# Adding a bias row and a layer's output to the residual with accumulating transfers begun on GpSimd

## The chip, the cores and the metric

The kernel runs on one core of one Trainium2 chip. The metric is device time in microseconds of one execution of the whole program. The engines of the core are TensorE (PE in the profile; its weight loads are PEld), VectorE (DVE), ScalarE (ACT), GpSimd (POOL) and SyncE (SP). Sixteen DMA engines move data between the on-chip memory and HBM, and inside the on-chip memory.

## The reference

Four graph attention layers run over `x` of shape (128, 64, 512), fp32, with one adjacency matrix of 64 x 64. Each is added to its input:

```
h = max(layernorm(x), 0);  x = x + layer_l(h)
layer 0: softmax(q k' / 8, masked) v                      8 heads of 64, q = h Wq + bq and so on
layer 1: the same, then @ Wo + bo
layer 2: r = adj' * (q k');  (r / |r| by rows) v          one head
layer 3: o = (masked softmax attention) @ Wp + bp;  o + layernorm(o) * gamma + beta
```

So in layers 0, 1 and 3 a row of 512 numbers (`bv`, `bo`, `beta`) is added to every row of the residual, and in layer 3 the projection's output `o` is added to the residual as well, beside its normalized form.

## The kernel before, in words

The 8192 rows are cut into 16 blocks of 512 rows (`NT` = 4 tiles of 128 partitions). The main loop takes all 16 blocks of layer 0, then those of layer 1, and so on: `n` runs from 0 to 63 with `l, k = divmod(n, 16)`. Between the layers a block's residual lies in HBM (`state`).

For each block, `load_x` brings the rows and `layer_norm` makes the transposed, normalized `hT`. The transposition is in `turn`: a DVE copy that splits the 32-bit words into halves (`z`), a transposing DMA issued on SP (`hp<-z`), and an ACT copy that joins the halves again. Projections are Strassen-like: seven products of 256 x 256 parts in place of eight, with sums of parts made on POOL (`S`, `SO`). `attend` makes scores, softmax and transposed weights (`s`, again with `turn`), and `finish0`, `finish13` multiply them with `v`.

`load_xo` loads the residual block a second time, into `xo`, and adds the row (`row`, a copy of the bias in every partition) with four POOL additions of 128 x 512. In layer 0 DVE then adds the attention's output to `xo`; in layer 1 the output projection adds its parts on DVE and POOL; in layer 3 `tail3` takes the finished output `o` tile by tile: statistics on DVE, `xo + o` on POOL, then on DVE two operations that add the normalized form, then the store. `o` lies in the one buffer named `kT`, which the key projection of another block writes next; the second last block has it in a weight buffer, `w`. The last block has a tail of its own in the main program, with its additions on DVE.

Nothing is issued when it is written in the source. Every operation is recorded as a step (`record`, `add`) with what it reads and writes, and `order` sorts all of them at the end: a list scheduler with a duration for each step from `duration`. Each engine takes the step of lowest rank that is ready by the plan's clock; a step on another engine may use a result `late` ns after its end. `port` and `PORT` model that DVE and POOL share a port. `issue` then writes the instructions in that order, and each engine runs its own list in order, with semaphores between engines. All of them therefore carry line 193 in the profile. Rotating buffers (`Ring`) are chosen while recording, so the order doesn't change them. PSUM has four buffers for projections (`mm`) and two for attention (`so`).

Of the kernel before, what the change touches and what calls it, by code (L numbers as in the profile page):

```python
# [15 lines left out]
ALU = mybir.AluOpType  # L16
AX = mybir.AxisListType

P = 128
G = 64  # L20
D = 512
KC = D // P
HD = 64
NT = 4
# [31 lines left out]
class Plan:  # L56
# [59 lines left out]
    def add(self, eng, calls, reads, writes, busy, late):  # L116
        i = len(self.steps)
        deps = {self.wrote[g] for g in reads | writes if g in self.wrote}
        for g in writes:
            deps |= self.readers.pop(g, set())  # L120
            self.wrote[g] = i
        for g in reads:
            self.readers.setdefault(g, set()).add(i)
        deps.discard(i)
        if eng == "tensor":
            self.products.append(i)
        elif eng == "sync" and len(self.products) >= AHEAD:
            deps.add(self.products[-AHEAD])
        self.steps.append((eng, calls, deps, busy, late))

    def order(self):
        n = len(self.steps)
        wait = [len(s[2]) for s in self.steps]
        users = [[] for _ in range(n)]
        for i, s in enumerate(self.steps):
            for d in s[2]:
                users[d].append(i)

        rank = [i - RUSH * any(v.tensor.name.startswith("mm_") for c in s[1] for v in c[1][1:] if isinstance(v, bass.AP)) for i, s in enumerate(self.steps)]
        ready = [0.0] * n  # L140
        free = {e: 0.0 for e in ("tensor", "vector", "scalar", "gpsimd", "sync")}
        moved = 0.0
        port = 0.0
        soon = {e: [] for e in free}
        here = {e: [] for e in free}
        for i in range(n):
            if not wait[i]:
                heapq.heappush(soon[self.steps[i][0]], (0.0, rank[i], i))
        out = []
        while len(out) < n:  # L150
            best = None
            for e in free:
                while soon[e] and soon[e][0][0] <= free[e]:
                    heapq.heappush(here[e], heapq.heappop(soon[e])[1:])
                if here[e]:
                    at = free[e]
                elif soon[e]:
                    at = soon[e][0][0]
                else:
                    continue  # L160
                if best is None or at < best[0]:
                    best = (at, e)
            at, e = best
            if not here[e]:
                while soon[e] and soon[e][0][0] <= at:
                    heapq.heappush(here[e], heapq.heappop(soon[e])[1:])
            i = heapq.heappop(here[e])[1]
            eng, _, _, busy, late = self.steps[i]
            if e == "sync":
                moved = max(moved, at + 1400) + late / 180  # L170
                late = moved + 600 - at - busy
            elif e == "vector" and late == PORT:
                busy += max(0.0, free["gpsimd"] - at)
                port = at + busy
            elif e == "gpsimd":
                busy += max(0.0, port - at)
            free[e] = at + busy
            out.append((at, i))
            for u in users[i]:
                same = self.steps[u][0] == e  # L180
                ready[u] = max(ready[u], at + busy + (0.0 if same and e != "sync" else late))
                wait[u] -= 1
                if not wait[u]:
                    heapq.heappush(soon[self.steps[u][0]], (ready[u], rank[u], u))
        self.start = {i: at for at, i in out}
        self.span = max(free.values())
        return [i for _, i in sorted(out)]
# [37 lines left out]
def duration(eng, op, aps, a, k):  # L225

    out = aps[0]
    n = out.free_size()
    if eng == "tensor":
        kdim, m = aps[1].partition_size(), aps[1].free_size()  # L230
        if op == "transpose":
            return 109, 200
        pass_ = max(n, P if m > HD else HD) * 0.842
        if m <= HD:
            pass_ = pass_ / (2 if kdim > HD else 4) + 1
        return 2 * pass_, 200
    if eng == "vector":
        n = max([n] + [v.free_size() for v in aps[1:]])
        if op == "bn_stats":
            return 590, 150  # L240
        if n <= HD:
            return 120, 150
        if out.dtype == U16:
            return 0.67 * n, PORT
        fixed = {"scalar_tensor_tensor": 140, "tensor_reduce": 100}.get(op, 85)
        two = sum("PSUM" not in str(v.space) and v.free_size() > HD for v in aps[1:]) > 1
        return fixed + n * 1.01, PORT if two else 150
    if eng == "scalar":
        own = isinstance(k.get("scale"), bass.AP)
        return max(240 + 0.49 * n, (1.32 if out.dtype == U16 else 1.4 if own else 0.95) * n), 170  # L250
    if eng == "gpsimd":
        if n <= HD:
            return (1010 if ALU.pow in a else 310), 120
        return n * (1.82 if n > D else 2.41), 120
    size = (2 if out.dtype == U16 else 4) * n * out.partition_size()
    return 1270 if k.get("transpose") else 520, size


@with_exitstack
def gnn_stack_kernel(  # L260
# [12 lines left out]
    pe, dve, act, gps = plan.tensor, plan.vector, plan.scalar, plan.gpsimd  # L273
# [28 lines left out]

    def dma(dst, src):
        plan.sync.dma_start(dst, src)

    def col(name, src):
        t = const.tile([P, KC], F32, tag=name, name=name)
        dma(t, src.rearrange("(c p) -> p c", p=P))
        return t
# [12 lines left out]
    def source(l, k):  # L322
        return xr[k] if l == 0 else state[l - 1][k]
# [112 lines left out]
    def stats(mv, t, src, nm):  # L436
        st = sm.tile([P, 6], F32, tag="st", name=f"st_{nm}_{t}")
        dve.bn_stats(st, src)
        dve.bn_aggr(mv[:, t, :], st)
# [6 lines left out]
    ready = set()  # L446
# [249 lines left out]
    def pieces(n, xo):  # L696

        l, k = divmod(n, NB)
        for g in range(2):
            at = slice(2 * g, 2 * g + 2)  # L700
            if l in (1, 3):
                yield xo[:, at, :], lambda d, at=at: d[at].rearrange("t p d -> p t d")
            else:
                yield xo[:, at, 0:H2], lambda d, at=at: d[at, :, 0:H2].rearrange("t p d -> p t d")
                for y in range(2):
                    yield (
                        xo[half(y), at, H2:],
                        lambda d, at=at, y=y: d[at, half(1 - y), H2:].rearrange("t p d -> p t d"),
                    )

    def store(n, xo):
        l, k = divmod(n, NB)
        for sb, dr in pieces(n, xo):
            dma(dr(target(l, k)), sb)

    xos = {}

    def load_xo(n):
        l, k = divmod(n, NB)
        xos[n] = p2.tile([P, NT, D], F32, tag="xo", name=f"xo_{n}")  # L720
        for sb, dr in pieces(n, xos[n]):
            dma(sb, dr(source(l, k)))
        yield 4
        if l in xo_row:
            row = R[xo_row[l]]
            for t in range(NT):
                gps.tensor_tensor(xos[n][:, t, :], xos[n][:, t, :], row, ALU.add)
                if t < NT - 1:
                    yield 1
        ready.add(("xo", n))  # L730

    def finish0(n):
# [118 lines left out]
    def tail3(n, o):  # L851

        xo = xos[n]
        mv = sm.tile([P, NT, 2], F32, tag="mv", name=f"mvo_{n}")
        rs = sm.tile([P, NT], F32, tag="rs", name=f"rso_{n}")
        yield 1
        for t in range(NT):
            stats(mv, t, o[:, t, :], f"o{n}")
            gps.tensor_tensor(xo[:, t, :], xo[:, t, :], o[:, t, :], ALU.add)
            yield t % 2  # L860
        pow_mhalf(rs, mv[:, :, 1], LN_EPS, f"o{n}")
        yield 1
        for t in range(NT):
            a = p4.tile([P, D], F32, tag="z", name=f"a_{n}_{t}")
            dve.scalar_tensor_tensor(a, o[:, t, :], mv[:, t, 0:1], R["gam"], ALU.subtract, ALU.mult)
            dve.scalar_tensor_tensor(xo[:, t, :], a, rs[:, t : t + 1], xo[:, t, :], ALU.mult, ALU.add)
            yield 1
        yield 1
        store(n, xo)
# [138 lines left out]
    for n in range(N):  # L1008
        l, k = divmod(n, NB)
# [14 lines left out]
        if l != 2:  # L1024
# [12 lines left out]
            if l == 0:  # L1037
                spawn(load_xo(n), 2)
# [30 lines left out]
    for t in range(NT):  # L1069
# [10 lines left out]
        o, xo = o3[:, t, :], xos[m][:, t, :]  # L1080
        dve.tensor_tensor(o, ps, R["bp"], ALU.add)
        stats(mv, t, o, "last")
        at = slice(t, t + 1)
# [41 lines left out]
```

## Time and profile before

| | us |
|---|---|
| median of 3 runs (lowest, highest) | 2844.2 (2843.95, 2844.62) |
| the profiled execution's own time | 2844.57 |
| span in its trace, first to last instruction | 2842.8 |
| busy in that span: PE | 2828.4 |
| DVE | 2037.6 |
| POOL | 1840.5 |
| ACT | 1248.0 |

The profile's groups are named by what they write and read, with buffer numbers left out: `xo<-xo,row` is the addition of a row to the residual, `hp<-z` a transposing DMA, `so<-v,s` and `so<-s,v` the attention products, `mm<-...` the projections. Weight loads overlap products. Issuing a DMA is not counted as busy time of the engine that issues it; such an entry carries a q (SPq). Matmuls are pipelined and their groups overlap, so that a group's mean duration times its count exceeds its busy time.

### The profile page before, as it was taken

The page shows a single profiled execution, that of the slowest core. Times are in us where ns is not written, and L with a number is a line of the kernel's source. Part 1 is how long each engine was busy: PE and PEld are TensorE (multiplying, and loading weights), DVE is VectorE, ACT ScalarE, POOL GpSimd, SP SyncE. Part 2 cuts the span into 40 slices and gives each one's busy share as a digit, 9 for nine tenths or more (in the row PEclk, how much of TensorE's full clock was granted, in tenths as well). Part 3 has the DMA queues.
Part 4 walks back from the last instruction along what each step waited for, and adds up shares of the span by engine and source line. Part 5 has one row for each costly group of instructions (what it writes and reads, how often), then busy time and mean ns, then how long its engine had stood idle before and what let it go on. Part 6 is the DMA issues. An engine that isn't in the chain of part 4 may idle for free.

```text
span 2842.8 us, 62036 instructions
## 1 busy us (share of the span) xinstructions
PE 2828.4 (99%) x25833; PEld 2471.6 (87%) x25833; DVE 2037.6 (72%) x3104; ACT 1248.0 (44%) x1589; POOL 1840.5 (65%) x1349
## 2 busy tenths in 40 slices
PE   9999999999999999999999999999999999999998
PEld 8878888888888888888888888888888888888887
DVE  7767778876767767667666555555688888778787
ACT  4555555454443534534434343443444444444442
POOL 6555566656766667667677334344678687787796
PEclk9999999999999999999999999999999999999999
DMA  6766666556453533533546565756433433433432
GB/s 158 163 137 156 143 146 134 127 128 163 105 120 80 124 95 82 131 85 86 136 114 156 136 162 143 164 128 157 120 86 94 119 86 95 112 91 96 109 84 66
DMA packets 634890, 342.29 MB, mean 120 GB/s; under 512 B 485232, under 2 KB 566384, under 8 KB 634608
## 3 DMA queue, kind: packets, MB, share of 16 engines
q1 hardware_dynamic: 634608, 338.32, 50.0%
q8 instruction: 202, 3.31, 0.5%
q14 instruction: 80, 0.66, 0.1%
HBM read 152.61 MB, written 69.21 MB: 78 GB/s over the span
## 4 chain that ended last, share of the span: by engine, by line
PE 96%; DVE 3%; issue 0%; POOL 0%; DMA 0%; ACT 0%; POOLq 0%; SPq 0%; DVEq 0%
PE mm L193 88%; PE so L193 8%; DVE z L193 1%; DVE st L193 0%; POOL s L193 0%; DVE u L193 0%; DVE sr L193 0%; DVE kT L193 0%; DMA xin<-in_x_dram 0%; DVE mv L193 0%; DVE w L193 0%; DVE xo L193 0%; ACT xin L193 0%; ACT oT L193 0%; POOLq L1120 0%
## 5 line engine op out<-in xcount | busy, mean ns | idle before, releaser
L193 PE MATMUL mm<-S,w 128*128 128x256 f32 x3584 | 817.2, 380 | 0.0
L193 PEld LDWEIGHTS mm<-S,w 128*128 128x128 f32 x3584 | 679.3, 190 | 93.8 <-issue 1.0
L193 PE MATMUL mm<-hT,w 128*128 128x256 f32 x2688 | 629.9, 380 | 4.0 <-DVE kT L193 3.7
L193 DVE TENSOR_TENSOR u<-mm,s 128x512 f32<-128x512 f32 x414 | 284.9, 688 | 480.1 <-PE mm L193 342.3
L193 PEld LDWEIGHTS mm<-hT,w 128*128 128x128 f32 x2688 | 509.6, 190 | 75.5 <-DVE kT L193 5.3
L193 PE MATMUL mm<-w,S 128*128 128x256 f32 x2048 | 472.8, 381 | 0.0
L193 PEld LDWEIGHTS mm<-w,S 128*128 128x128 f32 x2048 | 385.5, 190 | 53.8 <-issue 0.5
L193 ACT COPY hT<-hp 128x1024 uint16<-128x1024 uint16 x252 | 332.7, 1350 | 90.3 <-DMA hp<-z 90.2
L193 PE MATMUL mm<-w,hT 128*128 128x256 f32 x1536 | 366.4, 381 | 0.0
L193 ACT COPY s<-hp 128x1024 uint16<-128x1024 uint16 x188 | 252.3, 1352 | 204.3 <-DMA hp<-z 197.1
L193 ACT COPY s<-mm 128x512 f32<-128x512 f32 x211 | 123.0, 583 | 490.0 <-PE mm L193 419.0
L193 POOL TENSOR_TENSOR s<-s,mx 128x1024 f32<-128x1024 f32 x96 | 183.3, 1911 | 226.9 <-DVE mx L193 224.9
L193 PEld LDWEIGHTS mm<-w,hT 128*128 128x128 f32 x1536 | 289.2, 190 | 40.2 <-DVE v L193 0.2
L193 POOL TENSOR_TENSOR xo<-xo,row 128x512 f32<-128x512 f32 x192 | 286.1, 1510 | 8.4 <-DMA xo<-in_x_dram 5.7
L193 DVE COPY z<-s 128x1024 uint16<-128x1024 uint16 x188 | 278.2, 1501 | 6.7 <-POOL s L193 6.6
L193 DVE COPY z<-xin 128x1024 uint16<-128x1024 uint16 x252 | 245.3, 988 | 37.6 <-ACT xin L193 34.0
L193 ACT ACTIVATE xin<-xin,nb,rs 128x512 f32<-128x512 f32 x256 | 195.4, 808 | 90.5 <-DVE nb L193 89.9
L193 PE MATMUL mm<-w,SO 128*128 128x256 f32 x992 | 224.3, 379 | 0.0
L193 POOL TENSOR_TENSOR qT<-u,z 128x512 f32<-128x512 f32 x64 | 87.5, 1367 | 202.2 <-DVE u L193 189.8
L193 PEld LDWEIGHTS mm<-w,SO 128*128 128x128 f32 x992 | 188.5, 190 | 25.6
L193 POOL TENSOR_TENSOR s<-s,sr 128x1024 f32<-128x1024 f32 x96 | 187.3, 1963 | 34.2 <-DVE sr L193 32.1
L193 ACT ACTIVATE s<-s 128x1024 f32<-128x1024 f32 (+1 forms) x112 | 108.1, 966 | 200.3 <-POOL s L193 144.3
(98 smaller groups left out, 3667.7 us busy)
## 6 DMA issues: line engine op xcount, KB each, us to landing
xin<-x SPq DMA_DIRECT2D x192, 256.0 KB, 4.0
xo<-x SPq DMA_DIRECT2D x64, 512.0 KB, 4.5
xin<-in_x_dram SPq DMA_DIRECT2D x64, 256.0 KB, 3.2
x<-xo SPq DMA_DIRECT2D x64, 256.0 KB, 2.5
x<-xo SPq DMA_DIRECT2D x128, 128.0 KB, 2.5
x<-xo SPq DMA_DIRECT2D x32, 512.0 KB, 3.0
out_dram<-xo SPq DMA_DIRECT2D x30, 512.0 KB, 3.0
xo<-in_x_dram SPq DMA_DIRECT2D x32, 256.0 KB, 3.2
```

Of the source, the lines that this page charges most:

```text
L193: getattr(getattr(self.nc, eng), op)(*a, **k)
```

## The change

The four row additions of a block become one accumulating DMA of 128 x 4 x 512 elements, issued on GpSimd's queue: `xo += row`, where the row is repeated four times by the access pattern. In `tail3`, the four additions of the output become one accumulating DMA of 128 x 2048 elements, recorded after the statistics of the last tile. The scheduler learns that a DMA may be issued by GpSimd: a step behind it on the same engine waits for its landing if it uses its result, and `duration` gives such a transfer 1100 ns on GpSimd and `2000 + size / 180` ns to landing. Steps of the last block's own tail stay as they are.

```diff
-            eng, _, _, busy, late = self.steps[i]
+            eng, calls, _, busy, late = self.steps[i]
+            moves = calls[0][0] == "dma_start"
+            if e == "gpsimd":
+                busy += max(0.0, port - at)
             if e == "sync":
                 moved = max(moved, at + 1400) + late / 180
                 late = moved + 600 - at - busy
             elif e == "vector" and late == PORT:
                 busy += max(0.0, free["gpsimd"] - at)
                 port = at + busy
-            elif e == "gpsimd":
-                busy += max(0.0, port - at)
...
-                ready[u] = max(ready[u], at + busy + (0.0 if same and e != "sync" else late))
+                ready[u] = max(ready[u], at + busy + (0.0 if same and not moves else late))
...
-    if eng == "gpsimd":
+    if eng == "gpsimd" and op != "dma_start":
...
     size = (2 if out.dtype == U16 else 4) * n * out.partition_size()
+    if "accum_op" in k:
+        return 1100, 2000 + size / 180
     return 1270 if k.get("transpose") else 520, size
...
+    def add(dst, src):
+
+        gps.dma_start(dst, src, accum_op=ALU.add)
...
             row = R[xo_row[l]]
-            for t in range(NT):
-                gps.tensor_tensor(xos[n][:, t, :], xos[n][:, t, :], row, ALU.add)
-                if t < NT - 1:
-                    yield 1
+            add(xos[n], row.unsqueeze(1).to_broadcast([P, NT, D]))
+            yield 3
         ready.add(("xo", n))
...
             stats(mv, t, o[:, t, :], f"o{n}")
-            gps.tensor_tensor(xo[:, t, :], xo[:, t, :], o[:, t, :], ALU.add)
+            if t == NT - 1:
+                add(xo, o)
             yield t % 2
```

## The prediction

> **What bounds the kernel now.** I read the page's engine row first, then the list of PE's waits, then the groups by form, then the timeline of one layer-0 block. The engine row:
>
> ```profile
> span 2842.8 us, 62036 instructions
> PE 2828.4 (99%) x25833; PEld 2471.6 (87%) x25833; DVE 2037.6 (72%) x3104; ACT 1248.0 (44%) x1589; POOL 1840.5 (65%) x1349
> ```
>
> PE is busy for all but 14.4 us of the span. The list of PE's waits (engine, line, waited for: us in total, times, longest) says how little of that is a wait:
>
> ```profile
> PE mm L193 <- DVE kT L193: 3.7, 4, 0.9
> PE mm L193 <- POOL ident masks.py:199: 1.3, 1, 1.3
> ```
>
> All its entries sum to 6.4 us; the rest is the head and the tail. The 3.7 us are four stalls of 0.9 us in layer 3, where DVE, held up beside POOL, emptied a PSUM bank late. So whatever leaves POOL or DVE can give back about 4 us, and anything that makes PE wait is paid in full. The groups that the change touches (busy us, mean ns of one, idle before):
>
> ```profile
> L193 POOL TENSOR_TENSOR xo<-xo,row 128x512 f32<-128x512 f32 x192 | 286.1, 1510 | 8.4 <-DMA xo<-in_x_dram 5.7 <-DMA xo<-x 2.7
> L193 POOL TENSOR_TENSOR xo<-xo,kT 128x512 f32<-128x512 f32 x56 | 80.8, 1472 | 0.0
> L193 POOL TENSOR_TENSOR xo<-xo,w 128x512 f32<-128x512 f32 x4 | 6.3, 1605 | 0.0
> L193 ACT COPY s<-hp 128x1024 uint16<-128x1024 uint16 x188 | 252.3, 1352 | 204.3 <-DMA hp<-z 197.1 <-DVE mv L193 5.8 <-DVE u L193 0.9
> q1 hardware_dynamic: 634608, 338.32, 50.0%
> ```
>
> ACT's copy of a transposed attention tile waits 197 us for the transposing DMA: that DMA is the last step before the attention product. The DMA engines are half busy; by stretches it is 0.63 in layer 0 (42 to 760 us), 0.45 in layer 1 (760 to 1560), 0.38 in layer 3 (2010 to the end). In one layer-0 block (start, length, engine):
>
> ```profile
> 518.32 2.91 SPq L193 DMA_TRANSPOSE hp<-z  x2
> 522.55 4.63 POOL L193 TENSOR_TENSOR xo<-xo,row 128x512 f32<-128x512 f32 x3
> 526.49 2.61 SPq L193 DMA_TRANSPOSE hp<-z  x2
> 531.91 1.37 ACT L193 COPY s<-hp 128x1024 uint16<-128x1024 uint16 x1
> 536.55 2.10 PE L193 MATMUL so<-v,s 64*64 64x64 f32 x128
> ```
>
> The last attention copy ends at 533.28 and the attention product starts at 536.55: a margin of 3.3 us, with the row additions standing among the very transposes that fill it. Measured so in the timeline for each block, the margin is 0.8 to 3.3 us in layer 0 (mean 2.1), 1.8 to 3.5 in layer 1 (2.4), and 0.4 to 3.7 in layer 3 (1.5). PE runs in a fixed order, so a tile later than that stops it.
>
> **What the Trainium skill says.** "DMA: Bandwidth & Descriptors", Anatomy of one DMA (SWDGE path): a transfer begun on GpSimd takes about 2.0 us plus bytes at 436 GB/s. The same page, Issuing engines are not separate DMA queues: transfers of all engines share the same 16 DMA engines and interleave. "Collectives: The Full Stack", The bandwidth ceiling: an add inside the DMA needs two source reads on one read ring and so runs at about half the rate of a copy. "SBUF — State Buffer", Who interferes with whom: GpSimd writes the descriptors through the port it shares with VectorE, so a VectorE copy can hold them up. The trace of before has no transfer begun on GpSimd, so the first and third can't be checked. That DVE copies and POOL block each other it shows: the copy z<-s takes 0.7 us alone and up to 1.9 beside POOL (group mean 1501 ns against 988 for the same copy z<-xin).
>
> **The change, part by part.** *Removed from POOL:* 192 row additions (286.1 us) and 60 output additions (80.8 + 6.3), 373 us of its 1840.5. None ends PE's waits, so nothing comes back there except part of the four stalls of 0.9 us: I count -3 us.
>
> *Added to POOL:* 63 transfers of 1 MB, 48 of the row (16 blocks in each of layers 0, 1 and 3) and 15 of the output. What POOL is held for one is not shown. Below it is bounded by SP's DMA issue, 0.58 us (median); above by the four additions it replaces, 6.0 us. I take 1.1 us, the value by which the changed plan lays its order (69 us in all), against the page's 2.0 us for everything fixed, most of which it puts at completion.
>
> *Landing.* Two reads of 1.05 MB at 436 GB/s are 4.8 us on all 16 engines, so 6.8 us on idle engines (estimate from the two pages). At layer 3's share of 0.38 the 4.8 us stretch to 7.7 and the landing to 9.7 us. The plan assumes 1.1 + 7.8 = 8.9. The bound below is 4.4 us (one read); above I take 15, twice the plan's. Altogether 63 x 4.8 = 302 us of all engines, 50% to about 61%.
>
> *Moved.* Instruction counts on PE, DVE, ACT and SP stay; PE's order changes in few places, mostly neighbouring products swapped. What was spread in four pieces is now one burst, and SP's transposes share the engines with it. Queue by queue:
> - Layer 0: the row transfer stands on POOL just after qT<-u,z, where the block above has its additions (522.55), with the four attention transposes issued from 518 to about 530. The burst takes up to 4.8 us from them; I take 4.1, near the top, because transposes stand before and behind it in SP's queue. Less the margin of 2.1 this is 2.0 us of PE per block, x16 = 32 us. Bounds: 0 (it fits into the idle 37%) and 4.8 - 0.8 = 4, x16 = 64.
> - Layer 1: the row transfer stands before the two s<-s,sr multiplications, so half of the burst is over when the first transpose comes: 2.4 us against a margin of 2.4. I take 0.25 x16 = 4; bounds 0 and 16 x 1.5 = 24. The addition's user, DVE xo<-mm,xo, came 5.9 us after POOL's last row addition before; the transfer starts earlier and covers that.
> - Layer 3, row: the same place, margin 1.5: 0.5 x15 = 8; bounds 0 and 35.
> - Layer 3, output: the transfer waits for all of o. Behind it, DVE has before the first xo<-z,rs,xo: 6 statistics with aggregates at 0.79 us, 4 z<-kT at 0.75, two u<-mm at 0.6, nb: about 9.3 us. Landing at 9.7 leaves DVE waiting 0.4 us; behind it stand qT<-mm,u and the z<-xin copies, PE's next banks and the next block's hT. I take 0.5 x14 = 7; bounds 0 and (15 - 9.3) x14 = 80. The next writer of o's one buffer, ACT kT<-mm, comes some 13 us after o's last write (2505.5 to 2518.4), beyond the landing. The wait for the store falls behind this and hides in SP's idle time (SP waited 490 us for DVE xo).
>
> What covers POOL's 1.1 us is the time that the removed additions left. If it were longer, the s<-s,sr behind it in layers 1 and 3 would be late, and with them the copies, transposes and attention product.
>
> **The sum.** 32 + 4 + 8 + 7 - 3 = +48 us on the profiled execution's 2844.57 (span 2842.8 and 1.8 around it), which lies 0.4 above the median 2844.2: 2892 us.
>
> **The rivals.**
> - *Hidden, not slower.* The bursts fit into the engines' idle time, the margins hold and the stalls of 0.9 us shrink. For it: margins of 2 us everywhere and a DMA share of 0.4 to 0.6. Against: in layer 0 the transfer meets the transposes in every block. It decides where the burst delays the last transpose by less than about 1 us in layer 0. 2841 to 2849 us. Chance 0.14; in a fifth of it just faster by over 0.2%, which would need more than the waits listed, from the ends of the span.
> - *POOL is held longer.* The row transfer is 512 pieces of 2 KB, and DVE's copies shut the port. At 4 us POOL is late by 2.9 in front of s<-s,sr: less margins of 2.4 and 1.5, about 0.5 x16 + 1.4 x15 = 29 us more, and as much again where ve, rs and nb stand behind the output's transfer (1.5 x14 = 21): 2940. At 6 us 2 more per block on 45 blocks: 3030. For it: nothing in this trace prices it. Against: POOL has gained 373 us. Chance 0.26.
> - *The addition is slow in the DMA engines* (landing 13 to 15 us). In layer 3 DVE waits 4 to 6 us x14 with two banks' time (2 us) of it hidden by PE's lead, 28 to 56 us more: 2920 to 2950, and transposes suffer longer, up to 3000. Chance 0.15.
> - *It doesn't do what it says:* excluded for the most part, since the built order has all 63 transfers in place of the 252 additions.
>
> **How the numbers follow.** About 0.2% (5.7 us) is what a measurement can tell from no change. My case (2850 to 2920) has 0.44, hidden 0.14, POOL held 0.26, slow addition 0.15, and 0.01 is left over. Faster 0.03; same 0.11 (the rest of hidden); slower 0.86. The likeliest is 2892. The range reaches from hidden, 2842, to POOL held for nearly 6 us, 3015; about one in ten lies above and one in twenty below.
>
> **What would show it.** Right: PE waits for ACT s<-hp by some 2 us a block in layer 0, few in layer 1; ACT waits longer than 197 us for hp<-z; POOL busy near 1500 us; DMA share up by about 10 points. In layer 3, DVE xo<-z,rs,xo ends less than 1 us after its transfer. Wrong: no new PE waits (hidden); POOL's transfers of several us with s<-s,sr late (second rival); DVE xo waiting many us for xo<-kT (third).

## The result, and the profile after

The changed kernel takes 2891.22 us (median of 4 runs, 2884.75 to 2896.02) against 2844.07 for the kernel before (the three runs above and one more): ratio 1.0164, 95% interval 1.0151 to 1.0176, slower by 47 us. The profiled execution is the shortest of the four, 2884.75 us with a span of 2882.9, so its own account has to explain 40 us and not 47.

The page of the changed kernel, engines and DMA queues:

```profile
span 2882.9 us, 61996 instructions
PE 2840.5 (99%) x25833; PEld 2476.4 (86%) x25833; DVE 1933.2 (67%) x3104; ACT 1241.7 (43%) x1589; POOL 1559.0 (54%) x1160
...
q1 hardware_dynamic: 634608, 338.32, 50.7%
q0 software_dynamic: 27504, 66.06, 13.3%
...
xo<-row POOLq DMA_DIRECT2D x48, 1024.0 KB, 8.4
...
xo<-kT POOLq DMA_DIRECT2D x14, 1024.0 KB, 7.1
```

POOL lost 281 us of work. DVE lost 104 us; its copy `z<-s` fell from 1501 to 1263 ns, less often held up beside POOL. Neither was the bound. The 63 transfers (queue q0) take 13.3% of the DMA engines. Still PE looks 99% busy: its busy time grew by 12 us, most of which the clock explains below.

PE's waits (engine, line, waited for: us in total, times, longest):

```profile
PE mm L194 <- DVE u L194: 7.1, 3, 5.8
PE so L194 <- ACT s L194: 6.0, 3, 3.8
PE mm L194 <- ACT kT L194: 5.2, 2, 4.7
PE mm L194 <- DVE kT L194: 5.0, 2, 3.2
PE mm L194 <- ACT z L194: 3.2, 1, 3.2
PE mm L194 <- ACT hT L194: 2.4, 1, 2.4
```

All entries of the list sum to 34.2 us, against 6.4 before: +27.8. The timeline puts practically all of the new ones before 800 us, in layer 0 and its end; layer 3's four stalls of 0.9 us are gone. Only the second entry is the attention product that I had named. The others are projections whose PSUM bank or operand came late from DVE or ACT. Who held those up, in the waits of layer 0 alone (42 to 770 us):

```profile
ACT s L194 <- DMA hp<-z: 104.4, 34, 10.5
...
DVE z L194 <- DMA hp<-z: 70.8, 22, 11.8
ACT hT L194 <- DMA hp<-z: 62.1, 31, 6.7
```

Before, in layer 0 (42 to 760 us), ACT waited less than half as long for the same DMAs, and DVE 3.1 us in all:

```profile
ACT s L193 <- DMA hp<-z: 43.6, 22, 5.5
...
ACT hT L193 <- DMA hp<-z: 26.9, 24, 3.1
```

The transposes landed late (landing is the moment when all data of a transfer has arrived). In layer 0, first before, then after:

```profile
DMA to landing us min/median/max: 3.0/3.2/6.4
...
DMA to landing us min/median/max: 3.0/3.8/16.3
```

One block shows the whole course (the timeline, engine by engine: start, length, engine, operation, and in brackets the idle time before it and what ended it):

```profile
421.03 1.65 POOL L194 DMA_DIRECT2D xo<-row  x1
...
421.83 8.26 SPq L194 DMA_TRANSPOSE hp<-z  x2
...
431.30 1.89 PE L194 MATMUL mm<-w,hT 128*128 128x256 f32 x8
...
437.63 0.69 DVE L194 COPY z<-s 128x1024 uint16<-128x1024 uint16 x1 [11.78 <-DMA hp<-z]
437.68 1.34 ACT L194 COPY s<-hp 128x1024 uint16<-128x1024 uint16 x1 [10.52 <-DMA hp<-z]
438.24 0.68 DVE L194 TENSOR_TENSOR u<-mm,s 128x512 f32<-128x512 f32 x1
...
438.98 3.78 PE L194 MATMUL mm<-w,S 128*128 128x256 f32 x8 [5.79 <-DVE u L194]
```

POOL begins the transfer at 421; SP needs 8.3 us to issue two transposes, which take 1.2 us each otherwise; ACT stands 10.5 us and DVE 11.8 us before a step that needs a transposed tile or the buffer `z` that the transpose still reads. The PSUM evacuation `u<-mm,s` (it takes a finished product out of its bank) stands behind that step on DVE, and PE stops for 5.8 us.

The last line shows a second cost: eight products in 3.78 us, where eight of the same shape took 1.89 just before the stall. Busy time by stretches (PE busy, PEld, DVE, ACT, POOL, then PEclk, DMA share, GB/s):

```profile
415.00:436.00 21.00, 18.19 (x85) 15.67 (x83) 9.21 (x16) 4.88 (x8) 7.29 (x5) 1.00 1.00 121
437.20:443.90 6.70, 4.92 (x52) 3.73 (x56) 5.00 (x9) 3.28 (x3) 1.26 (x1) 0.50 1.17 167
444.00:470.00 26.00, 26.00 (x324) 22.90 (x317) 20.53 (x30) 14.86 (x20) 17.09 (x12) 1.00 0.51 130
```

PE's clock is granted at half (0.50) after the stall. The clock records show five such stretches, four of 3.4 us and one of 6.8, together 20.5 us at half clock. PE stood still in 2.4 us of these; the 18.1 us in which it worked cost half of that, 9 us. Waits and clock make 27.8 + 9 = 37 of the 40 us. The other 3 lie in PE's busy time (it grew by 12, of which the clock is 9), and I can't place them.

### The profile page after: what moved, and what is told of

It is laid out like the page before. It is cut to its first block, busy times and chain, and to the rows that moved or that the text cites. A ratio compares the mean times of both kernels' runs of the same rounds, so it can differ in the third digit from the quotient of the medians.

```text
span 2882.9 us, 61996 instructions
## 1 busy us (share of the span) xinstructions
PE 2840.5 (99%) x25833; PEld 2476.4 (86%) x25833; DVE 1933.2 (67%) x3104; ACT 1241.7 (43%) x1589; POOL 1559.0 (54%) x1160
## 3 DMA queue, kind: packets, MB, share of 16 engines
q0 software_dynamic: 27504, 66.06, 13.3%
## 4 chain that ended last, share of the span: by engine, by line
PE 91%; DMA 5%; DVE 2%; ACT 1%; issue 1%; POOL 0%; SPq 0%; POOLq 0%; ACTq 0%; DVEq 0%
PE mm L194 84%; PE so L194 7%; DMA hp<-z 4%; DMA xin<-in_x_dram 1%; ACT s L194 1%; DVE z L194 0%; ACT hT L194 0%; POOL s L194 0%; DVE sr L194 0%; DVE s L194 0%; ACT xin L194 0%; DVE st L194 0%; DVE kT L194 0%; DVE mx L194 0%; DVE xo L194 0%
## 5 line engine op out<-in xcount | busy, mean ns | idle before, releaser
L194 DVE COPY z<-xin 128x1024 uint16<-128x1024 uint16 x252 | 236.2, 952 | 113.9 <-ACT xin L194 60.5
L194 DVE COPY z<-s 128x1024 uint16<-128x1024 uint16 x188 | 233.5, 1263 | 26.5 <-DMA hp<-z 24.0
L194 POOL TENSOR_TENSOR s<-s,sr 128x1024 f32<-128x1024 f32 x96 | 201.5, 2224 | 34.0 <-DVE sr L194 31.1
L194 POOL TENSOR_TENSOR S<-hT 128x512 f32<-128x512 f32 x126 | 163.8, 1300 | 102.9 <-ACT hT L194 102.9
```

The source lines that it names most:

```text
L194: getattr(getattr(self.nc, eng), op)(*a, **k)
```

## The experiments

Each ran beside the kernel before, which took 2844.5 to 2844.7 us. "The theory" is that a transfer in the DMA engines beside the transposes slows them.

**Layer 0 back on POOL.** Edit:

```diff
-            add(xos[n], row.unsqueeze(1).to_broadcast([P, NT, D]))
-            yield 3
+            if l == 0:
+                for t in range(NT):
+                    gps.tensor_tensor(xos[n][:, t, :], xos[n][:, t, :], row, ALU.add)
+                    if t < NT - 1:
+                        yield 1
+            else:
+                add(xos[n], row.unsqueeze(1).to_broadcast([P, NT, D]))
+                yield 3
```

> Layer 0 has its four POOL row additions again; layers 1 and 3 and the output addition stay accumulating transfers (47 of 63). Theory (layer 0's transfer burst starves the transposes, all of the loss is there): the whole loss goes, 2838 to 2846 us, and if the 0.9 us stalls of layer 3 stay away, 2840. Rival (POOL's new steps and their place in its queue cost time in every layer): about 15 of the 47 us stay or more, 2855 to 2885 us.

2843.99 us, ratio 0.9998 (0.9990 to 1.0007). The 47 transfers in layers 1 and 3 cost nothing that can be measured, and gain nothing either.

**Layer 0 alone.** The reverse: `add` for l == 0, POOL's additions for the other rows and for the output.

> Only layer 0 has accumulating transfers (16 of 63); all else is on POOL as before. Theory (layer 0's burst): all of the loss or slightly more, 2885 to 2900 us. Rival (loss spread over layers, or over all POOL transfers): 16 of 63 of 47 us, about 2856 us.

2891.74 us, ratio 1.0170 (1.0155 to 1.0185), 47 us over before. Sixteen transfers make the whole loss.

**Layer 0 moved, first try.** Edit:

```diff
+        if eng == "gpsimd" and calls[0][0] == "dma_start" and self.hold and len(self.products) >= HOLD:
+            deps.add(self.products[-HOLD])
...
-        yield 4
+        yield 16 if l == 0 else 4
...
+            if l == 0:
+                spawn(load_xo(n))
             qT = p1.tile([P, KC, T], F32, tag="qT", name=f"qT_{n}")
```

`HOLD` is 6: the transfer also waits for the sixth last TensorE step recorded before it.

> All 63 transfers stay, but layer 0 loads its residual at the start of the block and issues the row transfer in the gap between the stores and the attention transposes, so that by the plan 9 instead of 47 transposes of layer 0 fall into a transfer. Theory (overlap with transposes): most of the loss goes, 2843 to 2860 us. Rival (the transfers cost POOL or the engines' time wherever they stand): 2880 to 2895 us.

2901.43 us, ratio 1.0207 (1.0178 to 1.0236). The expectation fell, but the trace shows that the kernel didn't do what it was made for: POOL came to the transfer after `qT<-u,z`, at 569.2 in one block, while SP issued six transposes from 559.8 to 576.8. Transfers and transposes shared 76.5 us of layer 0, as against 78 in the change (counted as in the table further below). The plan's clock is not the chip's. So this run decides nothing, neither for the theory nor for the rival.

**Layer 0 moved, second try.** The residual is loaded earlier, and the transfer is recorded in `attend` (no longer in `load_xo`), behind the second `s<-s,mx` and ahead of the `s<-s,sr` multiplications on POOL, where layers 1 and 3 have theirs:

```diff
+        if self.hold:
+            deps.add(max(j for j, st in enumerate(self.steps) if st[0] == "gpsimd"))
...
         yield 1
+        if l == 0:
+            plan.hold = True
+            add(xos[n], R["b0"].unsqueeze(1).to_broadcast([P, NT, D]))
+            plan.hold = False
         for s in ss:
...
+            if l == 0:
+                spawn(load_xo(n), 3)
             kT = p1.tile([P, KC, T], F32, tag="kT", name=f"kT_{n}")
```

> All 63 transfers stay whole; in layer 0 the residual is loaded earlier and the row transfer stands on POOL before the two s<-s,sr multiplications, as it does in layers 1 and 3, so that it is mostly over when the attention transposes start. Theory (overlap with transposes): 2845 to 2862 us. Rival (layer 0's transfers cost because the engines are fuller there, wherever they stand): 2880 to 2895 us.

2847.14 us, ratio 1.0009 (1.0000 to 1.0017). All 63 transfers are there, and 45 of the 47 us are gone. Layer 0 by stretch, columns as above, of this run and then of the changed kernel:

```profile
42.00:728.00 686.00, 682.09 (x6911) 589.05 (x6901) 486.71 (x776) 352.48 (x451) 347.02 (x249) 1.00 0.80 168
...
42.00:770.00 728.00, 696.42 (x6924) 598.99 (x6913) 487.87 (x780) 357.02 (x457) 352.25 (x249) 0.99 0.79 158
```

The DMA engines are as full as in the changed kernel (0.80 against 0.79) and PE stands still for 4 us in place of 32. The fullness of the engines was not the cause; the place of the transfer beside the transposes was. (The earlier load is part of this edit, and the order of the engines' lists shifts in places. The first try had both too and was no better for it.)

**Half of the transfer.** In layer 0 the transfer adds two tiles, POOL the other two: `add(xos[n][:, 0:2, :], ...)` and two `gps.tensor_tensor`.

> In layer 0 the transfer adds two of the four tiles, and POOL adds the other two; place as in the change. Theory (a burst starves the transposes, and the margin of some 2 us hides its first part): the burst is half of 7.3 us, the loss falls to well below half, 2846 to 2860 us. Rival (loss in proportion to bytes): 2865 to 2872 us.

2867.43 us, ratio 1.0080 (1.0064 to 1.0095): 23 us, half of the loss for half of the bytes, so the rival's figure and not mine. But not all of it lies in layer 0: in this order of instructions two row transfers of layer 1 met transposes and landed after 10.6 and 15.1 us, with stalls of PE of 1.7 and 2.1 us behind them and 1.7 us lost to the clock. Without these 5 us or so, layer 0 lost about 18, between the two figures. I had counted on the margin to hide a short burst.

**A plain copy.** Edit: `put` in place of `add` in layer 0, a `dma_start` without `accum_op`, in an unchanged order.

> Layer 0's transfer from GpSimd becomes a plain copy of the same 1 MB, same place and order: it leaves out the residual of layer 0 (the row replaces it). One read in place of two, packets of about 85 ns in place of 188. Theory (time in the engines beside transposes decides): the burst is half as long, and the loss falls to a third or half, 2855 to 2870 us. Rival 1 (any transfer on a second queue starves transposes alike): stays within 10 us of 2891. Rival 2 (only the adding in the DMA engine harms): back to 2841 to 2848 us.

2848.73 us, ratio 1.0012 (1.0005 to 1.0018), 4 us. Between two of my expectations, nearer to "only the adding harms". But this burst is shorter too: its packets are out within 3.8 us (median of the blocks) against 7.3. They were of 4 KB and took 168 ns, where I had expected 2 KB and 85 ns; per byte that is the same. So two copies next:

```diff
-            add(xos[n], row.unsqueeze(1).to_broadcast([P, NT, D]))
...
+                for d in (xos[n], spill):
+                    gps.dma_start(d, row.unsqueeze(1).to_broadcast([P, NT, D]))
```

> Layer 0's transfer becomes two plain copies of 1 MB behind each other, one into xo and one into a spare tile, in the change's own order of instructions: it leaves out the residual of layer 0. The engines are then taken for about as long as by the accumulating transfer (some 6 us in place of the single copy's 3), with no add in them. Theory (time in flight beside the transposes decides, whatever the transfer does): 2865 to 2895 us. Rival (adding in the DMA engines is what slows transposes): within 8 us of the single copy, 2845 to 2857 us.

2900.22 us, ratio 1.0198 (1.0182 to 1.0213), 56 us: more than my range, and far from the rival's. No add is needed for the loss. Two plain copies of 1 MB, whose packets are out within 7.8 us a block, do at least as much harm as one accumulating transfer with its two reads. That DVE, not only ACT, stands before the transposes is the same here; layer 0 of this run (42 to 790 us):

```profile
ACT s L194 <- DMA hp<-z: 117.2, 33, 12.4
...
DVE z L194 <- DMA hp<-z: 76.8, 20, 10.7
```

**Four tiles against four columns.** Both make four transfers of 256 KB of layer 0's one; in both the engines' lists are the same. The first edit is that of the tiles; in the columns the last line stands in place of its `add`.

```diff
+                plan.begin()
+                for t in range(NT):
+                    add(xos[n][:, t, :], row)
+                plan.end()
...
+                    add(xos[n][:, :, ts(t, P)], row[:, ts(t, P)].unsqueeze(1).to_broadcast([P, NT, P]))
```

> Layer 0's row transfer of 1 MB becomes four of 256 KB behind each other on POOL, one a tile, packets of 2 KB as before. Control for the run with columns, whose order of instructions is the same. All theories: the same number of packets beside the same transposes, 2880 to 2910 us (POOL is held about 4 us longer a block).

> As the four tiles, but each of the four takes a quarter of the columns of all tiles: packets of 512 B in place of 2 KB, four times as many, same bytes, same order. Theory of alternation (a transpose gets one 256 B packet for each accumulating packet, whatever its size): transposes get four times the turns in the same time, and the loss falls to a third or less, 2845 to 2870 us. Rival (the bytes read and written decide): within 8 us of the four tiles.

Tiles: 2875.66 us, ratio 1.0108 (1.0093 to 1.0123), somewhat under the expectation. Columns: 2893.05 us, ratio 1.0169 (1.0152 to 1.0186), 17 us more than the tiles. Alternation packet by packet falls, and so does the rival's figure (within 8 us). With packets of 512 B beside them the transposes did not get four times the turns but 207 packets a microsecond against 168. And the transfer itself was slower: 143 packets of 512 B a microsecond beside transposes, 73 GB/s, against 54 of 2 KB, 110 GB/s. GpSimd, too, was held longer for each, 2.2 us in place of 1.4, so the two runs do not differ in the packets alone.

**The output's transfer alone.** `add(xo, o)` stays; all rows are added on POOL.

> Only layer 3's output addition is by accumulating transfers (15 of 63); all rows are added on POOL as before. Theory: the stalls of 0.9 us in layer 3 go and nothing is added, 2839 to 2844 us. Rival (the transfer's landing holds DVE's last additions in layer 3): 2848 to 2860 us.

2855.16 us, ratio 1.0036 (1.0024 to 1.0049). My figure missed. The time lies in the rival's range, but not for the rival's reason. The trace shows a single event that costs most of it:

```profile
2124.77 14.62 SPq L194 DMA_TRANSPOSE hp<-z  x4
...
2129.16 0.94 POOL L194 DMA_DIRECT2D xo<-kT  x1 [1.64 <-DVE kT L194]
...
2148.58 1.13 PE L194 MATMUL so<-s,v 64*64 64x64 f32 x32 [8.28 <-ACT s L194]
2150.82 1.13 PE L194 MATMUL so<-s,v 64*64 64x64 f32 x32 [1.11 <-ACT s L194]
```

In this order of instructions the output's transfer of one block in layer 3 starts at 2129.2 among four transposes; it lands 17.8 us later, a transpose of this layer needs as much as 17.8 us, and PE stops for 8.3 us. DVE does wait 7.9 us for the transfer, as the rival has it, but PE waits for ACT's copy of the late transposed tile, the wait that I had named for layer 0. The clock is at half for 10.2 us, in 5.1 of which PE works, which costs 2.5. In the changed kernel the 14 like transfers met next to no transposing packets (60 in all) and landed in 6.9 to 7.8 us. So layer 0 is not special. But not every meeting costs: ten others of this run's 14 transfers met 240 to 860 transposing packets each (the costly one 1012), landed in 7.5 to 10.4 us, and PE's stalls beside them were of 1.2 us at most. The runs don't separate how much falls together from which tile is late.

**What orders the runs.** In each trace I counted the half microseconds of layer 0 in which both transposing packets and packets begun on GpSimd start (more than three of each). The losses are of the whole run; in four tiles, half and four columns, some 5 us of them lie in layer 1, where row transfers landed late in all three:

| kernel | shared time in layer 0, us | over before, us |
|---|---|---|
| layer 0 on POOL | 0 | -0.7 |
| moved, second try | 13 | 2.6 |
| one plain copy | 25.5 | 4.1 |
| four tiles | 42.5 | 31 |
| half | 46.5 | 23 |
| two plain copies | 75 | 56 |
| layer 0 alone | 75.5 | 47 |
| moved, first try | 76.5 | 57 |
| the change | 78 | 47 |
| four columns | 85.5 | 49 |

The order is rough, as four tiles and half show, but it holds in the main: up to 26 us shared cost 4 us at most, 42 to 47 cost 23 to 31, and 75 or more cost 47 to 57.

Within the shared time of the change, transposes make 109 packets a microsecond, against 546 without a transfer beside them. The transfer makes 59, against 81 without a transpose. A transpose has 1024 packets, so five times slower means some 9 us in place of 2. SP's own loads and stores do far less: before, they share 78 us of layer 0 with transposes by the same count, and the transposes still make 367 packets a microsecond. Those follow one another in one queue, however, and no run began the transfer on an engine other than GpSimd, so whether any second queue would do it stays open. Why transposes lose so much more than their share of bytes or of packets is not settled: alternation by packet was tried and fell.

## Why the prediction was right, and where it was not

The forecast was 2892 us and the result 2891. The place of most of the loss and its mechanism were right: a burst beside layer 0's transposes, tiles late, PE stopped in its fixed order. That the sum came within 1 us is luck: layer 0's term was 15 us too small, the three terms of layers 1 and 3 were some 19 too large, and the gain of 3 didn't show.

- *Layer 0, +32.* Measured 47 (layer 0 alone). The term was too small in two ways. The step "the burst takes up to 4.8 us from them" assumed that transposes lose no more than the transfer's own time on the engines. The transfer's packets took 7.3 us in layer 0 to get out, and transposes beside them ran at a fifth of their rate, so that the latest landed after 16.3 us. And the half clock after a stall was in no step: 9 us of the profiled 40 here, 14 of the 47 in the run with layer 0 alone.
- *The path.* I named the wait of the attention product for ACT, some 2 us in each block. It is 6.0 of the 34.2 us of PE's waits, in 3 places, and PE did not lose a little in each block: eight stalls of 1.8 to 5.8 us in 16 blocks make 27 of the 34 us. I had not followed what is queued behind a late transpose on DVE: the copy into a `z` buffer that the transpose still reads, and behind it the PSUM evacuations. "Who waits behind the waiting instruction" had to be asked of DVE's buffers as well.
- *Layers 1 and 3, +4, +8 and +7.* Measured nothing (-0.7 us for the 47 transfers, interval of about -2.8 to +2). The step that failed is "half of the burst is over when the first transpose comes": the row transfers of these layers land in 8.0 us, with nearly all of their packets out before the first transposing packet. Some 1600 transposing packets, about one and a half transposes' worth, met all 47 transfers of these layers together; in layer 0, some 11,600 met 16. For the output, DVE waited 0.7 us in all for `xo<-kT`; it landed in 7.1 us where I had 9.7.
- *The gain, -3.* The stalls of 0.9 us did go in the trace (all waits of PE are 4.6 us with layer 0 back on POOL, 6.4 before), but the total doesn't show it beyond its interval.
- *POOL.* Taken at 1.1 us a transfer; measured 1.39 for the row (512 pieces) and 0.90 for the output: 80 us in all where I had 69. The rival of POOL held for 4 us is out. So is the landing of 13 us and more, except where transposes stand beside the transfer (up to 18.2 us in layer 0). The prediction's reading that a copy `z<-s` takes up to 1.9 us is low, the longest took 2.4; no term rested on it.
- *Engine time.* The estimate of 4.8 us from the Trainium skill ("DMA: Bandwidth & Descriptors", Anatomy of one DMA, with the two source reads of "Collectives: The Full Stack", The bandwidth ceiling) was near for the output and low for the row. A plain packet of 2 KB takes 84 ns, an accumulating one 188, somewhat more than twice; 32 of these for each engine are 6.0 us. The output's packets of 8 KB make 8 x 641 ns = 5.1 us. The share of the engines rose by 14 points, not 11.
- *"They interleave"* (the Trainium skill, "DMA: Bandwidth & Descriptors", Issuing engines are not separate DMA queues) holds here, since packets of both start in the same half microseconds, and misled me to equal shares, of which that section says nothing. Here the measurement decides: the transposes keep a fifth of their rate, the transfer three quarters of its own.

## What to carry to other kernels

Before work is moved from an engine with slack into a DMA, look at what else is in the DMA engines at that moment, and not only at their mean share: the same 63 transfers cost 47 us in one place of the queue and 3 us in another, at the same share of the engines in layer 0. A DMA transpose on the way to a matmul is a bad neighbour to meet with a transfer of a megabyte. And where one engine is 99% busy with 6 us of waits in all, work taken from another engine can bring next to nothing: the 47 transfers of layers 1 and 3 alone took POOL's busy time from 1840.5 to 1632.5 us (the run with layer 0 back on POOL), and the time stayed where it was.

## What the runs showed of the hardware that was not expected

- A transpose beside a transfer of 1 MB begun on GpSimd is slowed about fivefold (109 against 546 packets of 256 B a microsecond), and SP is held up in issuing the next ones: up to 6.2 us for one, where 1.2 is usual. Plain copies do it too, to 133 packets a microsecond in the run with two.
- After five PE stalls of 2.4 to 5.8 us the clock was granted at half, for 3.4 us or twice that (10.2 us in two other runs). Not after every such stall: one of 3.2 us was not followed by it. The Trainium skill ("TensorE: Matmul & The Clock Gate", Part 1: The HAM clock gate) tells of a free-running activity window of that length, which fits the 3.4 us. It puts the half clock after at least one idle window of about 3.4 us; here stalls shorter than that were enough, 2.4 us in the changed kernel and 2.3 us in the run with half of the transfer, and the measurement decides.
- Accumulating transfers in packets of 512 B were slower in bytes than those of 2 KB, alone (230 packets a microsecond, 118 GB/s, against 77, 158 GB/s) as well as beside transposes.
